# A graph network's first message stage: 555 instead of 491 edge tiles counted, their one-hots made one tile at a time from SBUF, and the stage's side work spread over the counted tiles

## The chip, the core and the metric

The kernel runs on one core of a Trainium2 chip. The metric is the device time of one execution in microseconds, as the median of several runs. Engines are named as the profile names them: PE is the matrix engine (PEld its weight loads), DVE the vector engine, ACT the scalar engine, POOL the GpSimd engine, SP the queue that issues plain transfers.

## What is computed

A graph of 12,500 nodes with 32 features and 200,000 edges, sorted by destination, passes through two message layers:

```python
def _L0_gnn_ref(x, W, b, src, dst):
    out_norm = rsqrt(max(segment_sum(ones, src), 1))
    in_norm = rsqrt(max(segment_sum(ones, dst), 1))
    agg = segment_sum((x * out_norm[:, None])[src], dst)
    return agg * in_norm[:, None] @ W + b

h = maximum(layernorm(x), 0)
x = x + _L0_gnn_ref(h, W, b, src, dst)
h = maximum(layernorm(x), 0)
# per edge: relu MLP of [h_i, h_j - h_i], 64 -> 64 -> 128 -> 64 -> 32, mean over the edges of a destination
x = x + _L1_gnn_ref(h, src, dst, W1, b1, W2, b2, W3, b3, W4, b4)
```

All arithmetic is to float32 accuracy; the first layer keeps it with three bfloat16 terms per value.

## The kernel before

Edges come in tiles of 128 and chunks of four tiles (512 edges); there are 391 chunks. The program is one instruction stream per engine in an order written out by hand (`tc.manual_schedule()`); each engine runs its stream in that order, and waits on the others through semaphores.

**Stage A** (until about 338 us): layer norm, the table `tab_h` of normalized rows, the out-degrees of all nodes, and the scaled table `tab_hn` (three bfloat16 terms and a one per node). Meanwhile POOL gathers the source rows of the first 64 chunks (`EARLY`) from unscaled tables, one indirect transfer for each tile of 128 edges (line 211, the one line that issues all gathers).

**Stage B** (the first layer's sums, until about 1392 us) treats the chunks in three ways:

- The 64 early chunks hold rows without the degree factor. `scale_rows` looks the factor up on chip and adds the chunk: a transfer of `srow`, the compare `sturned` (line 656), twelve small products `look` (674), four `mask` instructions (681), the three bfloat16 terms `rows_scaled` (695, 697), the one-hot `hot_e`, four products (703), and an addition into the sums (562). It is a generator; `advance(running)` moves every running one by one stage per chunk step, and a new one starts every third chunk step (`LATER = 3`).
- Chunks 64 to 267 (below `DIR = 268`) are gathered from `tab_hn` by POOL, four gathers each into one of eight `rows` buffers, one-hots `hot` are made on DVE (624), and `sum_rows` (638) multiplies them on PE.
- The last 491 tiles (`ND`) from chunk 268 on are not gathered at all. `count_edges` makes, for each tile, a matrix of counts (source row within 128 by destination) from two one-hots on PE (786), `lo` and `oh`; ACT copies it from PSUM to SBUF as bfloat16 (788), in two parts, `count_two` and `count_third`, each with a single PSUM buffer; and after eight tiles (`TD`) `multiply` multiplies the on-chip `table` with the eight counts, 98 products (735) spread over the first five tiles of the next eight, then turns, places and adds the result (749, 754, 562).

`oh` is made on DVE for two tiles in one instruction (723): a comparison of `keys`, in SBUF, with `count_h`, which lies in PSUM:

```python
onehots[i // 2] = oh = dp.tile([P, 3, KW, 2], BF16, name="oh", bufs=4)
nc.vector.tensor_tensor(
    oh, keys[:, :, i : i + 2][:, :, None, :].to_broadcast([P, 3, KW, 2]),
    count_h[:, None, :, :].to_broadcast([P, 3, KW, 2]), op=OP.is_equal)
```

A step of the outer loop issues one chunk's gathers, then the steps of `count_edges` that are due (`stages = ND + 2 * TD = 507` spread over `steps = DIR - EARLY - 6 = 198` chunk steps), one step of the early chunks, and `sum_rows` of two chunks before. Node updates (`update_nodes`, some twelve stages each: product with the weights, norm, product with the next layer's weights, and the writes of `tab_j` and `tab_i` by SP) are queued when all edges of four node blocks are summed, and advance by one stage per counted tile.

**Stage C** (the second layer, to the end) can start gathering when the last update has written `tab_j`: 1563 gathers `gj` on POOL, and for each pair of chunks four PE stages `first` to `fourth` with lags of 1, 3, 4 and 5 steps.

Of the kernel before, what the change touches and what calls it, by code (L numbers as in the profile page):

```python
# [57 lines left out]
LATER = 3  # L58
# [6 lines left out]
DIR = 268  # L65
# [19 lines left out]
def gnn_kernel(  # L85
# [59 lines left out]
    keys = early.tile([P, 3, ND + 1], F16, name="keys")  # L145
# [140 lines left out]
    with tc.tile_pool(name="deg", bufs=3) as hp, tc.tile_pool(  # L286
# [105 lines left out]
        base_ps = pp.tile([P, ND], F32, name="base_ps")  # L392
        nc.tensor.matmul(base_ps, ones, base_f, start=True, stop=True)
        drel = hp.tile([P, ND], F32, name="drel", bufs=1)
        nc.vector.tensor_tensor(drel, dst_i[:, DIR * TPC : NTR], base_ps, op=OP.subtract)
        nc.vector.tensor_reduce(bounds[:, 0:1], drel, AX.X, OP.min)
        nc.vector.tensor_reduce(bounds[:, 1:2], drel, AX.X, OP.max)
        key = hp.tile([P, ND], F32, name="key", bufs=1)
        nc.vector.scalar_tensor_tensor(
            key, hl[:, 0, DIR * TPC : NTR], float(WD), drel, op0=OP.mult, op1=OP.add)  # L400
        nc.vector.memset(keys[:, :, ND:], 0.0)
        for k in range(3):
            nc.vector.tensor_scalar(keys[:, k, :ND], key, float(-KW * k), None, op0=OP.add)
# [54 lines left out]
    def update_nodes(pool, pp, q, sums_of):  # L458


        n = min(J, NBLK - J * q)
        at = slice(J * q, J * q + n)
# [8 lines left out]
        for j in range(n):  # L471
            parts_of = sums_of(j)
            for k, (part, w) in enumerate(parts_of):
                nc.tensor.matmul(ps[:, j, :], part, w, start=(k == 0), stop=(k == len(parts_of) - 1))
# [10 lines left out]
        for j in range(n):  # L485
            b = J * q + j
            nc.vector.scalar_tensor_tensor(
                x1[:, b, :], ps[:, j, :D], c[:, j : j + 1], x1[:, b, :], op0=OP.mult, op1=OP.add)
# [20 lines left out]
        ht = hts[q % 2]  # L509
# [8 lines left out]
        r = P * J * q  # L518
# [3 lines left out]
    class Sums:  # L522
# [43 lines left out]
        def block(self, q, j):  # L566
            return self.tiles[q][:, P * j : P * (j + 1)]
# [31 lines left out]
    with tc.tile_pool(name="e0", bufs=8) as sp, tc.tile_pool(name="nu", bufs=1) as np_, tc.tile_pool(  # L599
# [7 lines left out]

        def reached(g):
            return {q for q in (g // (GRP * J), (g + W // STEP - 1) // (GRP * J)) if q < NQ}

        missing = [len([g for g in range(NCH) if q in reached(g)]) for q in range(NQ)]

        def added(chunks):
            for g in chunks:
                for q in sorted(reached(g)):
                    missing[q] -= 1
                    if missing[q] == 0:
                        updates.append(update_nodes(np_, np_ps, q, lambda j, q=q: [(sums.block(q, j), w0t)]))
# [30 lines left out]
        def scale_rows(g):  # L649
# [4 lines left out]
            yield  # L654
            turned = sp.tile([PART, CHUNK], BF16, name="sturned", bufs=2)
            nc.vector.tensor_scalar(turned, row, part_s[:PART], None, op0=OP.is_equal)
            h = rows_early[:, g, :, :D]
            if g < RAW:
# [3 lines left out]
                nc.vector.tensor_sub(h, h, m[:, :, None].to_broadcast([P, TPC, D]))  # L662
                square = sp.tile([P, TPC, D], F32, name="raw_sq", bufs=2)
# [21 lines left out]
            if g < RAW:  # L685
# [4 lines left out]
                scaled, h, 0.0, w[:, :, None].to_broadcast([P, TPC, D]), op0=OP.max, op1=OP.mult)  # L690
            rows = sp.tile([P, TPC, D3], BF16, name="rows_scaled", bufs=2)
# [7 lines left out]
            yield  # L699

            total = ps[:D3, 1]
            for t in range(TPC):
                nc.tensor.matmul(
                    total, rows[:, t, :], hot[:, t // 2, :, t % 2], start=(t == 0), stop=(t == TPC - 1))
            adds.append((g, total))
# [9 lines left out]
        LATE = (TD - 3, TD - 2)  # L715

        def onehots_of(i):

            if i % TPC == 0:
                c = DIR * TPC + i  # L720
                los[i // TPC] = one_hots(dp, hl[:, 1, c : c + TPC], P, "lo", 3)
            onehots[i // 2] = oh = dp.tile([P, 3, KW, 2], BF16, name="oh", bufs=4)
            nc.vector.tensor_tensor(  # L723
                oh, keys[:, :, i : i + 2][:, :, None, :].to_broadcast([P, 3, KW, 2]),
                count_h[:, None, :, :].to_broadcast([P, 3, KW, 2]), op=OP.is_equal)
# [35 lines left out]
        def count_edges():  # L761
# [3 lines left out]
            onehots_of(0)  # L765
            onehots_of(2)
            for i in range(ND):
# [7 lines left out]
                if i % 2 == 0 and i + 4 < ND:  # L775
                    onehots_of(i + 4)
                oh, lo = onehots[i // 2], los[i // TPC]
# [3 lines left out]
                for ranges, name in ((THIRDS[:2], "two"), (THIRDS[2:], "third")):  # L781
# [3 lines left out]
                    for k in range(len(ranges)):  # L785
                        nc.tensor.matmul(  # L786
                            ps[:, k, :w], lo[:, i % TPC // 2, :, i % 2], oh[:, k0 + k, :w, i % 2], start=True, stop=True)
                    nc.scalar.activation(  # L788
                        counts[g][:, t, a:b, :].rearrange("p (k h) d -> p k (h d)", k=len(ranges)), ps[:, :, :w], AF.Copy)
# [10 lines left out]
        LAG = 2  # L800
        steps, stages = DIR - EARLY - 6, ND + 2 * TD
        for m in range(EARLY, DIR + LAG + 1):
# [3 lines left out]

            while adds:
                early, total = adds.pop()
                sums.add(slice(0, D3), STEP * early, total)
                added([early])  # L810
            if EARLY <= m - LAG - 1:
                add_rows(m - LAG - 1)
            i = m - EARLY
            slots = range(stages * i // steps, stages * (i + 1) // steps)
            for slot in slots:
                if next(counting, None) is None:
                    next(updating)
# [4 lines left out]
                advance(running)  # L822
                later, r = divmod(i, LATER)
                if r == 0 and later < EARLY:
                    running.append(scale_rows(later))
# [6 lines left out]
        assert not running and not updates and not any(missing)  # L832
# [4 lines left out]
    with tc.manual_schedule(), tc.tile_pool(name="prep", bufs=3) as prep, tc.tile_pool(name="e1", bufs=3) as ep, tc.tile_pool(name="fn", bufs=2) as fp, tc.tile_pool(  # L837
# [9 lines left out]
        def finish_nodes(q):  # L847
# [14 lines left out]
            for j in range(n):  # L862
                nc.tensor.matmul(po[:, j, :], sums.block(q, j), w4s, start=True, stop=True)  # L863
# [106 lines left out]
        last = 5  # L970
        for m in range(NPAIR + last):
# [170 lines left out]
```

## Time and profile before

| | us |
|---|---|
| median of 3 runs | 4361.06 (4347.4 to 4362.65) |
| profiled execution, own time | 3372.41 |
| its span, first to last instruction | 3370.4 |
| busy: PE, DVE, ACT, POOL | 2513.0, 1812.9, 1115.0, 2501.0 |

The profiled execution is shorter than the median of the runs by 989 us. Durations and waits are read from the profiled one. In its page, the second part shows the span in 40 equal slices of 84 us, one digit for the busy share in tenths; groups of instructions are listed by line with their count, their total and their mean; a wait names the engine that waited, and what released it.

### The profile page before, as it was taken

To read this page: it belongs to the slowest core of one execution; us is meant where nothing else is said; L and a number is where in the kernel's file an instruction comes from. 1 tells how busy PE (TensorE), PEld (TensorE's weight loads), DVE (VectorE), ACT (ScalarE), POOL (GpSimd) and SP (SyncE) were. 2 spreads that over 40 slices of the span, in tenths; PEclk is the share of its full clock that TensorE was granted. 3 is DMA by queue.
4 is the path that set the end of the run, shared out by engine and by line. 5 is a ranking of instruction groups with operands and counts; after the bars stand their busy time and mean duration, and the time that the engine had idled before them with its cause. 6 is when DMAs were issued, how large, how long until landed. Compare 5 with 4: busy or idle time off the path is not lost. (4 is left out here: it accounts for less than half of the span.)

```text
span 3370.4 us, 54101 instructions
## 1 busy us (share of the span) xinstructions
PE 2513.0 (75%) x20860; PEld 1782.4 (53%) x20860; DVE 1812.9 (54%) x4103; ACT 1115.0 (33%) x2029; POOL 2501.0 (74%) x2655
## 2 busy tenths in 40 slices
PE   3772888888888888477777777777776777777777
PEld 2660666667666666245455445445454544555544
DVE  7995788789878887233333333333333333333333
ACT  0002676677666775111212121121222121221121
POOL 7777777777777777477777777777777777777775
PEclk9855899999999999587878787888878787777788
DMA  4113112222222222222222222222222222222221
GB/s 98 15 15 79 27 28 34 31 37 34 34 34 34 33 35 49 44 59 63 59 59 64 60 62 59 63 59 63 59 62 60 59 63 59 63 59 62 60 60 31
DMA packets 234631, 170.64 MB, mean 51 GB/s; under 512 B 156008, under 2 KB 182856, under 8 KB 234368
## 3 DMA queue, kind: packets, MB, share of 16 engines
q0 software_dynamic: 84320, 75.96, 15.1%
q1 hardware_dynamic: 131306, 85.26, 9.7%
q10 hardware_dynamic: 18742, 5.89, 0.9%
q8 instruction: 168, 2.75, 0.3%
q14 instruction: 95, 0.78, 0.1%
HBM read 153.98 MB, written 12.92 MB: 50 GB/s over the span
## 5 line engine op out<-in xcount | busy, mean ns | idle before, releaser
L211 POOL DMA_INDIRECT gj<-tab_j,src_j x1563 | 1474.7, 944 | 506.9 <-issue 421.5
L211 POOL DMA_INDIRECT rows<-tab_hn,src_j x816 | 770.9, 945 | 252.4 <-issue 191.7
L937 DVE TENSOR_TENSOR h<-p,b3n 128x512 f32<-128x512 f32 x196 | 135.2, 690 | 738.2 <-PE p L934 738.2
L788 ACT ACTIVATE count<-count_two 128x858 bf16<-128x858 f32 x491 | 434.7, 885 | 282.0 <-PE count_two L786 255.7
L934 PE MATMUL p<-w3s,h 128*128 128x64 f32 x3128 | 444.7, 302 | 0.2 <-ACT h L926 0.2
L934 PEld LDWEIGHTS p<-w3s,h 128*128 128x128 f32 x3128 | 416.7, 215 | 48.3 <-issue 40.1
L926 ACT ACTIVATE h<-p,b2s 128x1024 f32<-128x1024 f32 x196 | 217.8, 1111 | 662.4 <-PE p L924 662.4
L902 PE MATMUL p<-gj,ident 128*1 128x8 f32 x392 | 39.1, 174 | 505.9 <-DMA gj<-tab_j,src_j 505.9
L735 PE MATMUL st<-count,table 128*128 128x104 bf16 (+1 forms) x6076 | 375.1, 217 | 48.4 <-ACT count L788 22.4
L735 PEld LDWEIGHTS <-table 128*128 128x128 bf16 x6076 | 347.7, 99 | 90.8 <-issue 30.6
L902 PEld LDWEIGHTS p<-gj,ident 128*1 128x1 f32 x392 | 21.7, 80 | 677.6 <-issue 664.1
L914 ACT ACTIVATE h<-p 128x512 f32<-128x512 f32 x196 | 117.0, 597 | 788.9 <-PE p L910 788.9
L723 DVE TENSOR_TENSOR oh<-keys,kept 128x2574 bf16<-128x2574 f16 x246 | 365.1, 1486 | 11.5 <-PE count_third L786 11.4
L952 PEld LDWEIGHTS ps<-hot,h 128*64 128x64 f32 x3126 | 272.4, 190 | 176.5 <-issue 165.1
L786 PE MATMUL count_two<-oh,lo 128*128 128x429 bf16 x982 | 277.3, 364 | 94.0 <-ACT count L788 84.1
L910 PE MATMUL p<-turned,ai 128*64 128x512 f32 x782 | 330.0, 936 | 0.0
L562 DVE TENSOR_TENSOR acc<-acc,ps 64x64 f32<-64x64 f32 (+1 forms) x198 | 44.7, 226 | 526.0 <-PE ps L952 493.4
L952 PE MATMUL ps<-hot,h 128*64 128x128 f32 x3126 | 298.0, 353 | 0.5 <-DVE h L937 0.5
L211 POOL DMA_INDIRECT rows_early<-tab_h,src_j x224 | 216.0, 964 | 71.2 <-issue 50.9
L886 DVE TENSOR_TENSOR turned<-row,kept 128x512 f32<-128x512 f16 x391 | 249.4, 679 | 26.8 <-PE p L910 22.0
L788 ACT ACTIVATE count<-count_third 128x416 bf16<-128x416 f32 x491 | 252.0, 513 | 0.0
L585 DVE TENSOR_TENSOR hot<-rel_h,kept 128x512 f32<-128x512 f16 x391 | 249.1, 678 | 0.0
(201 smaller groups left out, 3017.7 us busy)
## 6 DMA issues: line engine op xcount, KB each, us to landing
row<-rel_row SPq DMA_DIRECT2D x195, 256.0 KB
gj<-tab_j,src_j POOLq DMA_INDIRECT x1563
rows<-tab_hn,src_j POOLq DMA_INDIRECT x816
ai<-tab_i SPq DMA_DIRECT2D x195, 64.0 KB
srow<-hi_row SPq DMA_DIRECT2D x64, 98.0 KB
rows_early<-tab_h,src_j POOLq DMA_INDIRECT x224
tab_j<-nu_aij SPq DMA_DIRECT2D x24, 128.0 KB
tab_i<-nu_aij SPq DMA_DIRECT2D x24, 128.0 KB
```

The lines of the kernel that those rows point to most:

```text
L211: nc.gpsimd.indirect_dma_start(out=tile_ap, out_offset=None, in_=table, in_offset=bass.IndirectOffsetOnAxis(ap=col, axis=0))
L585: nc.vector.tensor_tensor(hot, rel_h[:, g * TPC : (g + 1) * TPC][:, :, None].to_broadcast([P, TPC, W]), lanes_f[:, None, :W].to_broadcast( ...
L723: nc.vector.tensor_tensor(oh, keys[:, :, i : i + 2][:, :, None, :].to_broadcast([P, 3, KW, 2]), count_h[:, None, :, :].to_broadcast([P, 3, ...
L735: nc.tensor.matmul(ps[:, : tiles * WD], table[:, h, :], c[:, :tiles, h, :], start=(h == 0), stop=(h == PART - 1))
L786: nc.tensor.matmul(ps[:, k, :w], lo[:, i % TPC // 2, :, i % 2], oh[:, k0 + k, :w, i % 2], start=True, stop=True)
L788: nc.scalar.activation(counts[g][:, t, a:b, :].rearrange("p (k h) d -> p k (h d)", k=len(ranges)), ps[:, :, :w], AF.Copy)
L886: nc.vector.tensor_tensor(turned, v["row"][:, k], part_f.to_broadcast([P, CHUNK]), op=OP.is_equal)
L910: nc.tensor.matmul(p1[k * HID : (k + 1) * HID].rearrange("p t e -> p (t e)"), v["ai"][:, k], v["turned"][k], start=False, stop=True, skip_ ...
L926: nc.scalar.activation(h2[:, :n], p2[:, :n], AF.Relu, bias=b2s)
L934: nc.tensor.matmul(p3[:, k * TPC + t, :], v["h2"][:, k, t * P : (t + 1) * P], w3s, start=True, stop=True)
L937: nc.vector.tensor_tensor(h3[:, :n], p3[:, :n], b3n[:, None, :].to_broadcast([P, n, HID]), op=OP.max)
L952: nc.tensor.matmul(ps[k * HID : (k + 1) * HID, o : o + W], v["h3"][:, k * TPC + t, :], v["hot"][k][:, t, :], start=(i == 0 and t == 0), st ...
```

## The change

`DIR` goes from 268 to 252: 64 tiles that were gathered are counted. The one-hot `oh` is made for one tile at a time, by a compare of a constant list of numbers in SBUF (`count_s`, 1287 to a partition) with the tile's key as a scalar for each partition; four are made ahead (`AHEAD_OH`), in seven buffers. The early chunks advance one stage per counted tile instead of per chunk step, start every eighth tile, and have more and shorter stages. The two halves of the node group `QD` are updated separately. Once all tiles are counted, five update stages are issued at a time (`QUICK`). In stage C the last pairs run with lags smaller by one.

```diff
-LATER = 3
+LATER = 8
-DIR = 268
+DIR = 252
...
-    keys = early.tile([P, 3, ND + 1], F16, name="keys")
+    key = early.tile([P, ND], F32, name="key")
+    count_s = early.tile([P, 3 * KW], F16, name="count_s")
...
-        base_ps = pp.tile([P, ND], F32, name="base_ps")
-        nc.tensor.matmul(base_ps, ones, base_f, start=True, stop=True)
-        nc.vector.tensor_tensor(drel, dst_i[:, DIR * TPC : NTR], base_ps, op=OP.subtract)
+        for c in range(0, ND, 512):
+            n = min(512, ND - c)
+            base_ps = pp.tile([P, 512], F32, name="base_ps")[:, :n]
+            nc.tensor.matmul(base_ps, ones, base_f[:, c : c + n], start=True, stop=True)
+            nc.vector.tensor_tensor(
+                drel[:, c : c + n], dst_i[:, DIR * TPC + c : DIR * TPC + c + n], base_ps, op=OP.subtract)
...
-            nc.vector.tensor_scalar(keys[:, k, :ND], key, float(-KW * k), None, op0=OP.add)
+            nc.vector.tensor_scalar(
+                count_s[:, KW * k : KW * (k + 1)], count_h[:, :, 0], float(KW * k), None, op0=OP.add)
...
+        units = [(J * q, min(J, NBLK - J * q)) for q in range(NQ) if q != QD] + [(J * QD, J // 2), (J * QD + J // 2, J // 2)]
...
             nc.sync.dma_start(row, bass.AP(
                 tensor=hi_row.tensor, offset=hi_row.offset + g * CHUNK, ap=[[0, PART], [1, CHUNK]]))
             yield
+            yield
             turned = sp.tile([PART, CHUNK], BF16, name="sturned", bufs=2)
...
                 nc.vector.tensor_sub(h, h, m[:, :, None].to_broadcast([P, TPC, D]))
+            yield
+            if g < RAW:
                 square = sp.tile([P, TPC, D], F32, name="raw_sq", bufs=2)
...
                 scaled, h, 0.0, w[:, :, None].to_broadcast([P, TPC, D]), op0=OP.max, op1=OP.mult)
+            yield
             rows = sp.tile([P, TPC, D3], BF16, name="rows_scaled", bufs=2)
...
             hot = one_hots(sp, rel_h[:, g * TPC : (g + 1) * TPC], W, "hot_e", 2)
             yield
+            yield
...
+            yield
             adds.append((g, total))
...
-            onehots[i // 2] = oh = dp.tile([P, 3, KW, 2], BF16, name="oh", bufs=4)
-            nc.vector.tensor_tensor(
-                oh, keys[:, :, i : i + 2][:, :, None, :].to_broadcast([P, 3, KW, 2]),
-                count_h[:, None, :, :].to_broadcast([P, 3, KW, 2]), op=OP.is_equal)
+            onehots[i] = oh = dp.tile([P, 3 * KW], BF16, name="oh", bufs=7)
+            nc.vector.tensor_scalar(oh, count_s, key[:, i : i + 1], None, op0=OP.is_equal)
...
-                if i % 2 == 0 and i + 4 < ND:
-                    onehots_of(i + 4)
+                if i + AHEAD_OH < ND:
+                    onehots_of(i + AHEAD_OH)
...
+        QUICK = 5
         steps, stages = DIR - EARLY - 6, ND + 2 * TD
...
             for slot in slots:
+                while adds:
+                    early, total = adds.pop()
+                    sums.add(slice(0, D3), STEP * early, total)
+                    added([early])
+                if slot == slots[0] and EARLY <= m - LAG - 1:
+                    add_rows(m - LAG - 1)
                 if next(counting, None) is None:
-                    next(updating)
+                    for _ in range(QUICK):
+                        next(updating)
+                later, r = divmod(slot - 3, LATER)
+                if r == 0 and later < EARLY:
+                    running.append(scale_rows(later))
+                advance(running)
...
+        def lags(m):
+            less = min(1, max(0, m - (NPAIR - 6)))
+            return [max(1, lag - less) for lag in (1, 3, 4, 5)]
```

## The prediction

> **What bounds the kernel now.** I read the page first, then its groups, the stretches, POOL's order of time, and PE's.
>
> ```profile
> span 3370.4 us, 54101 instructions
> PE   3772888888888888477777777777776777777777
> DVE  7995788789878887233333333333333333333333
> ACT  0002676677666775111212121121222121221121
> POOL 7777777777777777477777777777777777777775
> ```
>
> POOL is at 7 in every slice but the 17th (1350 to 1430 us). A 7 is its ceiling, as its own order of time shows:
>
> ```profile
> 1359.39 0.94 POOL L211 DMA_INDIRECT rows<-tab_hn,src_j  x1 [0.30 <-issue]
> 1360.63 0.94 POOL L211 DMA_INDIRECT rows<-tab_hn,src_j  x1 [0.30 <-issue]
> 1392.39 0.94 POOL L211 DMA_INDIRECT gj<-tab_j,src_j  x1 [30.81 <-DMA row<-rel_row]
> 1393.64 0.94 POOL L211 DMA_INDIRECT gj<-tab_j,src_j  x1 [0.31 <-issue]
> ```
>
> A gather takes 0.94 us and 0.30 us of issue: one each 1.249 us. So stage B is 816 x 1.249 = 1019 us of POOL, stage C 1563 x 1.249 = 1952 us, and between them POOL stands for 30.8 us, until the last update has written `tab_j`. But POOL isn't alone at its limit. In stage B the busy shares of PE and DVE are as high:
>
> ```profile
> 338.60:1326.70 988.10, 829.27 (x9741) 640.30 (x9742) 819.11 (x2267) 686.47 (x1320) 744.38 (x788) 0.96 0.21 33
> 1361.60:1392.40 30.80, 12.71 (x49) 9.51 (x49) 9.76 (x36) 4.92 (x13) 0.01 (x1) 0.50 0.13 31
> ```
>
> (PE, PEld, DVE, ACT, POOL, then the PE clock: 0.96.) In 988 us PE is busy for 829 and DVE for 819. From the first `count_third` product (323.2) to the last (1326.7) are 490 steps of 2.05 us. POOL offers one step per 1.95 us (198 chunk steps of 5.0 us for 507 steps), so the counting falls behind: `sum_rows` of a chunk comes 0.4 chunks after its gathers at chunk 82 and 7 at chunk 232, near the end of the eight buffers, and at 1117 and 1208 us a gather waits 0.6 and 2.3 us for a buffer. **Stage B has two bounds, a POOL pace and a counting pace, and the change moves 64 tiles from one to the other.** What counts is the counting pace, so I looked for its floor, in undisturbed groups of eight tiles:
>
> ```profile
> 806.74 0.35 PE L786 MATMUL count_third<-oh,lo 128*128 128x416 bf16 x1
> ...
> 814.98 0.54 PE L786 MATMUL count_two<-oh,lo 128*128 128x429 bf16 x2 [0.79 <-ACT count L788]
> 815.39 0.35 PE L786 MATMUL count_third<-oh,lo 128*128 128x416 bf16 x1
> ...
> 819.83 1.15 PE L735 MATMUL st<-count,table 128*128 128x104 bf16 x19 [0.79 <-ACT count L788]
> ...
> 821.20 0.35 PE L786 MATMUL count_third<-oh,lo 128*128 128x416 bf16 x1
> ```
>
> Eight tiles take 821.20 - 806.74 = 14.46 us; the next eight, to 835.48, take 14.28. That is **1.80 us per tile, with no wait for DVE in it**. It is made of PE alone in the first five tiles (three counting products and some 20 `st` products, 1.6 us), of a loop of PE and ACT in three (the single `count_two` buffer: 0.6 us of product, 0.89 of copy, 1.52 in all), and of 2.5 us where a group's products wait for its last copy. The other 0.25 us per tile of the mean are stalls:
>
> ```profile
> L723 DVE TENSOR_TENSOR oh<-keys,kept 128x2574 bf16<-128x2574 f16 x246 | 365.1, 1486 | 11.5 <-PE count_third L786 11.4
> ```
>
> ```profile
> PE st L735 <- DVE acc_d L558: 19.4, 9, 5.0
> ```
>
> DVE makes `oh` in blocks of 1.49 us; an early chunk's `mask` to `hot_e` is some 4 us in one piece (at 1299.8 to 1303.9), and the addition `acc_d` that frees the `st` buffer stands behind it: PE then waits up to 5 us.
>
> **The change part by part.** Times first in the profiled execution.
>
> *64 gathers fewer.* 64 x 1.249 = 80 us less POOL in stage B. Only what the counting pace allows of it is gained.
>
> *64 tiles more, and the one-hots.* Each tile costs the counting pace once. Does it fall to its floor? DVE's part: before, 1.41 us from start to start for two tiles, 0.70 per tile. The nearest row to the new compare is `sturned`, the same operation on 512 numbers in SBUF:
>
> ```profile
> L656 DVE TENSOR_SCALAR sturned<-srow,part_s x64: 343/347/564, 332.1 to 1321.3; 98x512 bf16<-98x512 f16 x64
> ```
>
> A compare by a scalar from PSUM (line 745, 160 numbers) takes 374 ns, 0.21 us beyond one number per cycle; with that, `sturned` leaves 0.135 us for 512, four per cycle. So 1287 numbers take 0.34 + 0.21 = 0.55 us, 0.47 from start to start: 0.23 less per tile. The other end: the Trainium skill, "VectorE: DVE Perf Modes", What auto-detection actually checks, gives the fast modes of one source where the outermost counts are both even or equal; 1287 is odd, but equal on both sides. If it ran at two per cycle, it would be 0.88 us, more than before. I take 0.55, the row of the same form. DVE's sum for eight tiles is then 8 x 0.47 for `oh`, 1.5 for `lo` and `hot`, 4.4 for an early chunk, 2.1 for places, additions and updates: 11.8 us in 14.4. It no longer limits, and its longest piece is about 2.6 us (masks and one `oh`) under four tiles made ahead. The early stages fall on fixed tiles of a group: `look` is issued after the eighth tile's products, where PE waits 0.8 us for ACT anyway; masks, terms and the four products have a tile each. I cost these moves at nothing; if the cover is gone they cost their old stalls, the 0.25 us per tile. The transfers of `srow` are 64 as before, one per eight tiles, issued a tile earlier; SP has room. PE's products read the same columns.
>
> So I take 1.80 us per tile: 555 x 1.80 = 999, the counts end at 323 + 999 = **1322** (before 1327, with 64 tiles less).
>
> *After the counts.* Before, 65.7 us pass from the last count to the first `gj`, as the gathers end at 1361.6 and three updates run one after another behind them (tab_j's writes at 1368.9, 1377.9 and 1388.5: 9 to 10.5 us each). After: the last two groups' products, 13.4 us as at 1326.7 to 1340.1; the update of the last three blocks, 9; the two halves, 7.3 each (10.5 less half of its products and wide instructions, 3.3); and 4 us from SP's issue to the gather. Sum 41. The first `gj` is at **1363** instead of 1392.4: 29 us saved. The early groups' updates lie in the counting (chunk 63 starts at tile 507). Two more writes by SP (0.36 and 0.5 us) lie in it.
>
> *The locks of POOL and DVE.* This is the rule that speaks against the change. At 1112.26 a `sturned` starts, and the gather that starts 0.10 us later takes 1.05 instead of 0.94; a gather under way made another `sturned` 0.53 long (754.12). The Trainium skill, "SBUF — State Buffer", Who interferes with whom, says that a DVE instruction in a two-port mode and GpSimd exclude each other for the whole instruction, and that the old form, one source in PSUM, stays out of it. If each of 555 compares held a gather for its 0.47 us, that were 261 us, and stage B would end near 1540. The trace prices it lower: a gather is delayed only where it starts 0.1 us or more after the compare and before its end less 0.13 us, that is for 0.33 of 1.249 us, by 0.17 on average: 0.04 us per compare, and at most as much again inside the gather: 24 to 42 us. By the trace POOL's part then ends at 338.6 + 939 + 24 to 42 = 1302 to 1320, 3 us later the last sum, 11 us later the first `gj`: 1316 to 1334, still ahead of 1363. So it costs nothing here, as the counting hides it.
>
> *Stage C* has the same 1563 gathers. Its end: 27.2 us pass from the last gather; a round of PE's four stages there is 4.0 us (3350.94 to 3354.95), and one lag less takes one away: -4. *Stage A* gains a product and makes `count_s` in three instructions of about 0.65 us for three of 0.41, under the early gathers: 0, at most 1.
>
> Sum: -29 - 4 = **-33 us**: 3339 of the profiled execution's 3372.41. The median of the runs is 1.293 times that, and no view says where its 989 us lie. If they are outside all of this, the gain stays 33 (4328); if all is stretched alike, 43 (4318); if they lie in the 2635 gathers (0.375 each), POOL alone bounds stage B, and 64 x 1.62 and the shorter gap count: 125 (4236). I take the middle one: **4318**.
>
> **The rivals.**
>
> *POOL becomes the only bound (0.22).* The counting goes below 1.74 us per tile, and the first `gj` comes at 1316 to 1334: with the end, 62 to 80 us saved, 4257 to 4281; the gathers' share of the 989 us leads to the same place or lower. For it: tiles go at 1.52 and 1.62 when nothing else is in the way. Against it: the floor of 1.80 has neither DVE nor POOL in it.
>
> *The counting doesn't speed up (0.28).* One mechanism: PE's order. Each wait of PE for a copy, an addition or an early product holds all tiles behind it, and 64 more pass through it. Decision point: 323 + 555p + 41 - 4 = 1392.4, p = **1.86**. At 1.93, half of the stalls left, it is 40 us slower: 4413; at the old 2.05, 106 slower, 4498. For it: PE's and ACT's work per tile is unchanged, the PE clock falls in stalls (0.96 in the mean), and five update stages in a row make PE wait for short chains. A compare at 0.88 us ends here too. Against: the stalls named above are DVE's, and their pieces become shorter.
>
> *It doesn't do what it says:* the tiles counted in eight-tile groups hide the one-hots anyway, so that only the gathers and the additional tiles count; that is p near 1.86 and no change, and lies between the first two.
>
> **How the numbers follow.** The likeliest case (0.50) is p from 1.76 to 1.85: -55 to -6 us, 4290 to 4353. By 0.5% (22 us, about what a measurement of this kernel can tell from no change) it is faster down from p = 1.825: 0.36 of the 0.50 faster, 0.13 same, 0.01 slower. The POOL case is all faster (0.22). The slow case is 0.24 slower and 0.04 same. Sum: faster 0.58, same 0.17, slower 0.25. The range leaves out a pace above 1.91 (about 0.14) and gains over 120 us: 4240 to 4402.
>
> **What would show it.** `oh` x555 at 0.55 us; the last `count_third` near 1322 with clean groups still at 14.3 us; the first `gj` near 1363, POOL's wait before it under 20 us or spread over waits for `rows` buffers; gathers in stage B mostly at 0.94 us, a quarter longer by up to 0.33; under 25 us from the last gather to the end. Wrong: `oh` at 0.88 us, counts ending after 1353, or groups well below 14 us.

## The result, and the profile after

The changed kernel takes 4358.65 us (median of 14 runs, 4333.5 to 4377.7) against 4352.0 us for the kernel before (14 runs, 4333.2 to 4367.1): a ratio of **1.0011, interval 0.9993 to 1.0028**. That is no change; predicted was 4318 us, a gain of 43 us.

The runs of a batch, before among them, lie together at one of two levels, near 4340 us or near 3380 us: the timed runs above are of the higher, and the profile of before shown ahead of the prediction (3372.41 us) is of the lower. So times and paces are compared at one level below, and both kernels have a profile at each: before_3 (4339.95 us) and before_again (3379.61 us), after_3 (4338.3 us) and after_4 (3378.9 us).

The page of the changed kernel, at the 4340 level:

```profile
span 4356.3 us, 56425 instructions
...
PE   2444277777777777773667777777777777777777
...
DVE  5555456555555555531222223222322222222323
ACT  0000255555555555550111111111111111111112
POOL 7554345445444444455566666666666666666663
```

In stage B (slices 6 to 18) POOL is at 4 to 5, where the page ahead of the prediction had it at 7, and PE stands at 7. That comes with the level and not with the change, as the page of the kernel before at this level, before_3, shows:

```profile
span 4337.9 us, 54101 instructions
...
PE   2444266677767777663577777777777777777778
...
POOL 6555355555555455555666666666666666666663
```

The order of time of POOL in the changed kernel at the turn from stage B to C, by start, duration, engine, line and what the engine waited for:

```profile
1963.44 0.94 POOL L212 DMA_INDIRECT rows<-tab_hn,src_j  x1 [0.30 <-issue]
1990.50 0.94 POOL L212 DMA_INDIRECT gj<-tab_j,src_j  x1 [26.12 <-DVE turned L902]
1991.75 0.94 POOL L212 DMA_INDIRECT gj<-tab_j,src_j  x1 [0.31 <-issue]
```

A gather still takes 0.94 us and 0.30 of issue; what the profile ahead of the prediction hardly had is the waiting between the gathers of stage B. These waits at this level, the kernel before first (engine and tile, what it waited for, us in total, times, longest):

```profile
POOL rows L211 <- PE ps_late L638: 399.2, 118, 7.8
```

and the changed kernel (after_3):

```profile
POOL rows L212 <- PE ps_late L644: 538.1, 166, 7.6
```

POOL stands for 400 to 540 us of a stage of 1490 until PE has summed the rows that occupy its buffers. At the 4340 level POOL is no bound in stage B; PE's order is. The counting itself, from the instructions that read `oh` (min/median/max in ns, first and last start), before_3:

```profile
L786 PE MATMUL count_third<-oh,lo x491: 344/349/552, 498.3 to 1905.7; 128*128 128x416 bf16 x164
L723 DVE TENSOR_TENSOR oh<-keys,kept x246: 1470/1490/1497, 496.0 to 1889.7; 128x2574 bf16<-128x2574 f16 x123
```

and after_3:

```profile
L737 DVE TENSOR_SCALAR oh<-count_s,key x555: 533/554/769, 497.3 to 1915.2; 128x1287 bf16<-128x1287 f16 x185
L798 PE MATMUL count_third<-oh,lo x555: 336/339/554, 498.6 to 1924.4; 128*128 128x416 bf16 x185
```

Before: 1407.4 us for 490 steps, 2.872 us per tile. After: 1425.8 for 554, **2.574 per tile**. So a tile did become 0.30 us cheaper, and the 64 additional ones took it back: to end where 490 steps had ended, 554 steps had to fall to 1407.4 / 554 = 2.540. The last count comes 18.7 us later. Behind it 24.7 us are saved (last count to first `gj`: 82.5 before, 57.8 after), and the first `gj` is at 1982.1 instead of 1988.2. Stage C is then as long as before, 2354 against 2350 us.

### The profile page after: what moved, and what is told of

Read it like the earlier page. It is cut to its first block, busy times and chain, and to the rows that moved or that the text cites. A ratio compares the mean times of both kernels' runs of the same rounds, so it can differ in the third digit from the quotient of the medians.

```text
span 4356.3 us, 56425 instructions
## 1 busy us (share of the span) xinstructions
PE 2992.5 (69%) x21798; PEld 2019.7 (46%) x21798; DVE 1747.1 (40%) x4444; ACT 1188.9 (27%) x2173; POOL 2466.6 (57%) x2591
## 4 chain that ended last, share of the span: by engine, by line
PE 46%; another core or an unknown queue 20%; issue 12%; ACT 10%; DVE 9%; POOL 3%; DMA 1%; ACTq 0%; DVEq 0%; POOLq 0%
PE p L950 9%; ACT count L801 8%; PE p L940 6%; PE count_two L798 5%; PE st L747 5%; PE ps L968 5%; PE p L926 5%; PE p L922 3%; POOL gj L212 3%; DVE lo L326 2%; PE count_third L798 2%; DVE hi L326 1%; PE ps_late L644 1%; DVE hot L587 1%
## 5 line engine op out<-in xcount | busy, mean ns | idle before, releaser
L950 PE MATMUL p<-w3s,h 128*128 128x64 f32 x3128 | 525.2, 328 | 169.6 <-issue 120.8
L950 PEld LDWEIGHTS p<-w3s,h 128*128 128x128 f32 x3128 | 486.1, 240 | 217.7 <-issue 156.9
L798 PE MATMUL count_two<-oh,lo 128*128 128x429 bf16 x1110 | 340.7, 393 | 312.4 <-ACT count L801 276.4
L747 PE MATMUL st<-count,table 128*128 128x104 bf16 (+1 forms) x6860 | 466.7, 224 | 68.7 <-issue 61.3
L747 PEld LDWEIGHTS <-table 128*128 128x128 bf16 x6860 | 419.3, 103 | 107.0 <-issue 80.3
L940 PE MATMUL p<-h,w2s 64*128 64x512 f32 x782 | 386.4, 887 | 79.2 <-issue 67.5
L798 PEld LDWEIGHTS <-lo 128*128 128x128 bf16 x1665 | 166.9, 107 | 447.3 <-issue 394.5
L737 DVE TENSOR_SCALAR oh<-count_s,key 128x1287 bf16<-128x1287 f16 x555 | 310.8, 567 | 51.4 <-remote 27.2
L343 PE MATMUL deg_ps<-hi,lo 128*128 128x98 bf16 x1563 | 183.5, 270 | 199.4 <-issue 140.4
L922 PE MATMUL p<-ident,gj 128*128 128x128 f32 x784 | 200.4, 371 | 116.1 <-issue 115.1
```

The costliest lines, as they stand in the source:

```text
L737: nc.vector.tensor_scalar(oh, count_s, key[:, i : i + 1], None, op0=OP.is_equal)
L747: nc.tensor.matmul(ps[:, : tiles * WD], table[:, h, :], c[:, :tiles, h, :], start=(h == 0), stop=(h == PART - 1))
L798: nc.tensor.matmul(ps[:, k, :w], lo[:, i % TPC // 2, :, i % 2], oh[:, KW * (k0 + k) : KW * (k0 + k) + w], start=True, stop=True)
L922: nc.tensor.matmul(p1[:, t, :], v["gj"][:, t].rearrange("p k c -> p (k c)"), ident, is_transpose=True, start=(t == 0), stop=False, skip_gr ...
L940: nc.tensor.matmul(p2[:, k], w2s[s, :], v["h1"][s, :], start=True, stop=True)
L950: nc.tensor.matmul(p3[:, k * TPC + t, :], v["h2"][:, k, t * P : (t + 1) * P], w3s, start=True, stop=True)
```

## The experiments

The theory after the result: *two bounds*. The new compare and the new order make a counted tile cheaper, and the 64 tiles eat it; the rivals were that compare and order are worth nothing, and that the gain is lost in stage C. Four expectations (a_oldoh, after_again, b_newoh, a_oldoh260) give their numbers mainly for one level, and the run fell on the other, so that these numbers were not put to the test there.

**before_again, before_3: the kernel before, unchanged.**

> The kernel before, unchanged, profiled once more, because its first profiled execution (3372 us) was 989 us shorter than every timed run. If the missing 989 us lie where the profile of the changed kernel shows its waits (TensorE issuing late, its signals coming late), then this profile is near 4350 us; theory 1 (the counting pace bounds stage B and the change made a tile cheaper, and the 64 additional tiles ate that): counting at 2.9 to 3.0 us per tile against 2.6 after, last count near 1940 in both. Theory 2 (neither the compare nor the schedule matters): 2.6 us per tile here too, last count near 1775, and the 165 us are lost elsewhere in stage B or in the gap to C. Theory 3 (gain in B, lost in C): last count after 1990, and stage C shorter here than the 2340 us of the changed kernel.

> The kernel before, profiled beside the next three. [...] Instruction theory: where before takes 4343, TensorE gets its instructions more slowly at regular places, some 965 us over 41,720 TensorE instructions (23 ns each), and the counting pace is 2.75 to 2.9 us per tile; POOL is then nowhere the bound in stage B. Where it takes 3378 it is as in before_again: 2.08.

before_again fell on the lower level, before_3 on the higher. At 4340 the counting pace is 2.87, close to theory 1's 2.9 to 3.0 (its last count, near 1940, comes at 1905.7); theories 2 and 3 (last count at 1775, or stage C longer after) fall. At 3380 it is 2.059, with POOL's gathers at 1.25 us and POOL the later bound.

**a_dir268: the change without its 64 tiles.** Run three times, as a_dir268, a_dir268_2 and a_dir268_3.

```diff
-DIR = 252
+DIR = 268
```

> The changed kernel with its 64 additional counted tiles taken back (491 tiles, 816 gathers in stage B), all else of the change kept. Theory 1: 64 tiles at 2.6 us are not paid: 130 to 170 us faster than before, near 4200. Theory 2 (the new compare and the order of stages are worth nothing, the tiles cost nothing either, POOL or something outside sets the time): within 0.5% of before, 4330 to 4370. Theory 3 (the additional tiles do save POOL's time as intended, and the new schedule loses it): slower than before by 64 gathers, 80 to 120 us, near 4450.

> Compare and order at 491 tiles, measured 32 us (0.9%) slower where before takes 3378, because its gathers are held up by the compares (41.7 us in sum). Where before takes 4340, POOL has slack in stage B: 25 to 40 us faster than before (0.6 to 0.9%), if the 64 tiles are what eats the gain of the other two parts. If instead the compare and the order don't add up (DVE's stalls can be taken away once only): 17 to 23 us, no more than the better of the two alone. If the 64 tiles cost nothing: within 0.2% of before.

> New compare and new order at 491 tiles. With before at 4340: if the 64 tiles are what eats the gain, 20 to 40 us faster than before (0.5 to 0.9%), the first gj 20 to 35 us earlier than the changed kernel's 1990; if the tiles cost nothing there, within 0.2%. With before at 3380: 27 to 32 us slower once more.

All three fell on the 3380 level: 31.7, 27.3 and 29.1 us *slower* than before (1.0094, 1.0082, 1.0084; intervals within 0.0016 of these). At this level theory 1's gain of 150 us isn't there, and its rival's loss is of a third of the size that it gave. What it is, b_newoh shows.

**b_newoh: the compare alone** (491 tiles, old order), at both levels.

```diff
-            onehots[i // 2] = oh = dp.tile([P, 3, KW, 2], BF16, name="oh", bufs=4)
-            nc.vector.tensor_tensor(
-                oh, keys[:, :, i : i + 2][:, :, None, :].to_broadcast([P, 3, KW, 2]),
-                count_h[:, None, :, :].to_broadcast([P, 3, KW, 2]), op=OP.is_equal)
+            onehots[i] = oh = dp.tile([P, 3 * KW], BF16, name="oh", bufs=7)
+            nc.vector.tensor_scalar(oh, count_s, key[:, i : i + 1], None, op0=OP.is_equal)
...
-                            ps[:, k, :w], lo[:, i % TPC // 2, :, i % 2], oh[:, k0 + k, :w, i % 2], start=True, stop=True)
+                            ps[:, k, :w], lo[:, i % TPC // 2, :, i % 2], oh[:, KW * (k0 + k) : KW * (k0 + k) + w], start=True, stop=True)
```

> The kernel before with one thing of the change alone: one compare per tile from SBUF (four ahead) in place of one per two tiles from PSUM; 491 tiles and the old order of stages. Lock theory: POOL is the later of the two bounds at 491 tiles, so the locks show in full: 25 to 40 us slower (0.7 to 1.2%), gathers of stage B longer by some 40 us in sum. Relief theory (DVE is what the counting waits for, and a shorter compare frees it): the same time or up to 15 us faster, as the last gathers wait less for the counting. Order theory (a_dir268's loss came from the new order of stages): within 0.3% of before.

> The compare alone at 491 tiles. Where before takes 4340: 17 us faster again (0.4%). Where it takes 3378: lock theory 25 to 40 us slower, with gathers of stage B longer by some 40 us in sum; relief theory equal or faster.

At 4340 it is 17.0 us faster (0.9957, 0.9944 to 0.9969), at 3380 it is 43.9 us **slower** (1.013, 1.0115 to 1.0145). The second is the lock theory's sign, and a little over its 25 to 40 us. The group of stage B's gathers (count, busy us and mean ns, idle before them), before_again:

```profile
L211 POOL DMA_INDIRECT rows<-tab_hn,src_j x816 | 772.2, 946 | 256.1 <-issue 193.9 <-DMA rows<-tab_hn,src_j 28.4 <-PE count_third L786 11.9
```

and b_newoh_2:

```profile
L212 POOL DMA_INDIRECT rows<-tab_hn,src_j x816 | 820.3, 1005 | 248.8 <-issue 189.7 <-DMA rows<-tab_hn,src_j 35.4 <-PE count_third L784 10.7
```

816 gathers of 1005 instead of 946 ns are 48.1 us more, and the last of them comes 42.8 us later (1408.0 for 1365.2). One such pair in its order of time:

```profile
505.14 0.56 DVE L723 TENSOR_SCALAR oh<-count_s,key 128x1287 bf16<-128x1287 f16 x1
505.24 1.27 POOL L212 DMA_INDIRECT rows<-tab_hn,src_j  x1 [0.30 <-issue]
```

The gather that starts 0.10 us after a compare takes 1.27 instead of 0.94. With the old compare in the new order (a_oldoh, a_oldoh264) the gathers are at 945 and 947 ns: it is the compare that lengthens them.

At 4340 the gathers are lengthened just so (1004 ns in b_newoh), but there POOL waits 337 us for PE's sums in any case, and what shows is that the counts end 24.0 us earlier than in before_3 (1881.7 for 1905.7). Whether that is relief of DVE is not shown: PE's waits for DVE in stage B fall only from 60.5 to 53.8 us. The edit has a second effect that the prediction put at nothing ("PE's products read the same columns"): the columns of `oh` that a product reads now lie side by side, and `count_third` takes 339 ns instead of 349, `count_two` 347 instead of 355 (medians). Over three products that is 0.026 us per tile, or 13 us for 491 tiles, by estimate half of the 24.

**a_oldoh, a_oldoh260, a_oldoh264, a_oldoh268: the order without the compare**, with 555, 523, 507 and 491 tiles. The edit to the changed kernel (also `keys` in place of `key` and `count_s`, and four buffers of `hot` instead of five, to make room; it is `count_h`, not `keys`, that lies in PSUM):

```diff
-            onehots[i] = oh = dp.tile([P, 3 * KW], BF16, name="oh", bufs=7)
-            nc.vector.tensor_scalar(oh, count_s, key[:, i : i + 1], None, op0=OP.is_equal)
+            onehots[i // 2] = oh = dp.tile([P, 3, KW, 2], BF16, name="oh", bufs=4)
+            nc.vector.tensor_tensor(
+                oh, keys[:, :, i : i + 2][:, :, None, :].to_broadcast([P, 3, KW, 2]),
+                count_h[:, None, :, :].to_broadcast([P, 3, KW, 2]), op=OP.is_equal)
...
-DIR = 252
+DIR = 268
```

a_oldoh keeps 252; 268 is a_oldoh268, and the other two have the number in their names.

> The changed kernel (555 tiles, new order of the early stages) with the one-hots made as before, two tiles in one compare against keys in PSUM, 1.49 us each; hot has four buffers instead of five to make room. Theory 1, with the compare as the source of the cheaper tile: 4430 to 4530 (555 tiles at 2.75 to 2.95). Theory 1, with the order of stages as the source: within 0.7% of after. Theory 2: within 0.5% of before.

> Change in its order of stages, but the old compare (no locks) and 523 tiles: the version that the runs so far point to. Lock theory with p = 1.9: 784 gathers at 1.26 to 1.30 end at 1327 to 1360, counts at 1316, first gj 17 to 25 us behind the last gather as in a_oldoh and a_dir268: 1350 to 1380 instead of before's 1397, and 4 us at the end: 20 to 50 us faster than before (0.6 to 1.5%). If the compare from SBUF is what speeds up the counting, p stays near 2.0 and it is within 0.5% of before or slower.

> The version with the old compare, the new order and 523 tiles, measured 8 us (0.2%) under before where before takes 4343. There again: the same. Where before takes 3378: instruction theory takes 21 us of extra cost away, so 25 to 35 us (0.7 to 1.0%) faster; lock theory, too, has it faster (20 to 50 us), and faster than the changed kernel; relief theory (the compare speeds the counting): within 0.5% of before, slower than the changed kernel.

> The new order of the stages (and of the updates and the last lags) alone: 491 tiles and the old compare of two tiles. If the order makes the tile cheaper (a_oldoh260 had 2.70 with 523 tiles, against 2.87 before): on a chip with before at 4340, pace 2.70 to 2.78, 15 to 30 us faster than before (0.4 to 0.7%). If the compare is what counts and a_oldoh260's pace was only the mixture of more tiles to fewer gathers: within 0.2% of before. On a chip with before at 3378: no locks, first gj 15 us nearer to the last gather: 10 to 25 us faster (0.3 to 0.7%) by the first, equal by the second.

> New order, old compare, 507 tiles and 800 gathers. Two bounds that cross: with before at 3380, gathers end at 338.7 + 800 x 1.25 to 1.28 = 1340 to 1363 and counts at 323 + 506 x 1.98 = 1325, first gj at 1366 to 1380 (a_oldoh268: 1384.8): 20 to 30 us faster than before (0.6 to 0.9%). If the bounds are blended, and more tiles only cost (a_oldoh, 555 tiles: 29 us slower): at or above a_oldoh268's 12 us gain, 3370 to 3380. With before at 4340: 8 to 20 us faster (0.2 to 0.5%), as it is 16 tiles from a_oldoh260 (5 and 8 us faster).

At 3380: 555 tiles 28.5 us slower (1.0079, 1.0064 to 1.0094), 491 tiles 11.7 faster (0.9964, 0.9951 to 0.9977), **507 tiles 16.8 faster (0.9944, 0.993 to 0.9957)**, the largest gain at this level, though its interval touches that of 491 tiles. a_oldoh's expectation gave only 4340's numbers, and the level was the other. In a_oldoh264 the gathers are of 947 ns again and end at 1337.9, the counts at 1303.7; its first `gj` at 1376.1 waits 37 us, in which the last updates run one after another behind the gathers. Its gain was put at 20 to 30 us and is a little under. At 4340, 523 tiles are 8.3 and 5.0 us faster (0.998, 0.9968 to 0.9992; 0.9987, 0.9973 to 1.0).

**b_dir260: the kernel before with 32 more tiles.**

```diff
-DIR = 268
+DIR = 260
```

> The kernel before with 32 more counted tiles (523) and nothing else of the change (the base product is cut in two so that it fits a bank). Theory 1: each tile costs its old pace, 2.9 to 3.0 us: about 94 us slower, 4440 to 4450. Theory 2: within 0.5%. Theory 3: faster by 32 gathers, 40 us or more, near 4310.

46.2 us slower at 3380 (1.0139, 1.0123 to 1.0154): 1.44 us for each tile, half of theory 1's 94 us. With the old compare and the old order, the counting is already close behind POOL, and more tiles only cost: POOL waits 99.5 us for PE's sums here. Its pace was not theory 1's 2.9, which belongs to 4340, but 1.997.

**a_dir260: the change with 523 tiles.**

```diff
-DIR = 252
+DIR = 260
```

> The changed kernel with 523 tiles, half way between 491 and 555. If a_dir268 was bound by POOL with its locks (816 gathers at 1.329) and the 555-tile kernel is bound by counting at p, then 784 gathers at 1.329 end at 341 + 1042 = 1383, 18 us earlier than a_dir268's: time 3392. If counting bounds it at 1.9: counts end at 322 + 994 = 1316 and don't matter. If both bounds are blended (each waits for the other in the one program order), it lies at or above the line between its neighbours. Where TensorE's pace alone bounds everything: 32 tiles at the pace of after less than after (60 to 83 us).

At 4340, 11.7 us faster than before (0.997, 0.9956 to 0.9985), where the changed kernel in the same batch is 8.3 slower: 32 tiles cost 20 us, 0.62 each, net of the 32 gathers they save. The expected 60 to 83 us, the tiles' full pace, missed: the pace rises to 2.676, by my reading because PE sums more gathered chunks among fewer counted tiles.

**after_again, after_3, after_4: the changed kernel beside these.**

> The changed kernel, unchanged, in the company of the next three. The run with the change but 491 tiles (a_dir268) had gathers longer by 41.7 us in all in stage B and its last one 35 us later; the run with the old compare (a_oldoh) counted at 1.907 us per tile against 2.08 of the kernel before. Lock theory: the compares from SBUF hold up gathers by 0.085 us each, but in this kernel POOL has slack, so that it doesn't matter; the counting pace decides. If the pace is that of a_oldoh (1.9: the order of stages makes it, the compare nothing), counts end at 1380 and the time is within 0.5% of before's. If the compare also helps (1.80, as predicted), counts end near 1322 and the time is 30 us (0.9%) under before's. If 2.05 as before: 3 to 4% slower.

> The changed kernel beside the kernel before. Instruction theory: the 64 tiles bring 1876 TensorE instructions; at 23 ns each that is 43 us where before takes 4343, and nothing where it takes 3378. So with 8 us more on the first sort of chip, the change must gain some 35 us (1.0%) on the second, as the prediction's sum of 33 has it. Pace theory (the pace stays at 1.9 to 2.05 and the gain isn't there on any chip): 0 to 4% slower on the second sort. Lock theory in its strong form: slower by 20 us or more on the second.

> The changed kernel beside the corners. Where before takes 4340: within 0.2% of before, and 25 to 45 us slower than a_dir268_2 (64 tiles at a net 0.4 to 0.7 us each, the counting bounding stage B and POOL not). Where before takes 3378: the prediction's sum has it 33 us faster; by the pace of a_oldoh (1.92) its counts end at 1385 and it is within 0.5%; as POOL isn't its bound there, the locks don't show in it, and it is faster than a_dir268 by 20 us or more.

At 4340: 8.3 us slower (1.0018, 1.0007 to 1.0028) and 0.9 slower (1.0004, 0.9987 to 1.0021). At 3380: 2.0 us faster (**0.9996, 0.9988 to 1.0004**). after_4's pace, 1.855, lies between the 1.80 of the prediction and the 1.9 of a_oldoh. So the change is worth nothing, within 0.3%, at either level, and the instruction theory, which wanted 35 us at 3380, falls there.

**a_probe: 2560 products more behind everything.**

```diff
+        for k in range(2560):
+            nc.tensor.matmul(probe_ps, probe, probe[:, :104], start=(k == 0), stop=(k == 2559))
```

> The changed kernel with 2560 products of the shape of st (128 x 104, each with its own load of weights) behind everything, in a row and waiting for nothing: 5120 TensorE instructions. Pace of such a row undisturbed: 0.05 us per product as in stage B's st, 140 us or so. Instruction theory: 140 us where before takes 3378; where it takes 4343 a further 23 ns per instruction, 118 us: 260 in all, in regular slow stretches, one each 256 instructions. If the slow chips lose their time in waits between engines, or in the clock, and not in supplying TensorE: 140 to 170 us on both sorts.

```profile
L1016 PE MATMUL probe_ps<-probe x2560: 209/209/210, 4326.8 to 4445.8; 128*128 128x104 bf16 x197
```

At 4340 the row takes 119.0 us, 46 ns for each product with its load; the kernel is 116 us longer than before (1.0264, 1.0225 to 1.0304). The instruction theory had 260 us for this level, and 140 for a row that isn't slowed: it falls here too. (At 3380 the row was not run.)

The runs side by side, difference to before in the same batch (us):

| tiles | compare | order | at 3380 | at 4340 |
|---|---|---|---|---|
| 491 | new | old | +43.9 | -17.0 |
| 491 | old | new | -11.7 | not run |
| 491 | new | new | +31.7, +27.3, +29.1 | not run |
| 507 | old | new | -16.8 | not run |
| 523 | old | old | +46.2 | not run |
| 523 | old | new | not run | -8.3, -5.0 |
| 523 | new | new | not run | -11.7 |
| 555 | old | new | +28.5 | not run |
| 555 | new | new (the change) | -2.0 | +6.7 (result), +8.3, +0.9 |

Which sign a part has depends on which bound is the later one. At 3380 in the new order, the new compare costs 39 us at 491 tiles (-11.7 to +27.3, in one batch), where POOL is the later bound, and gains 30 us at 555 (+28.5 to -2.0, in two batches), where the counting is: in a_oldoh POOL waits 174.9 us for PE's sums. So, too, the 64 tiles cost 40 us with the old compare (-11.7 to +28.5), and gain 29 with the new one (+27.3 to -2.0), as they take 64 gathers from a POOL that the compare has slowed. At 4340, where the counting is the bound throughout, the compare gains 17 us and 32 tiles cost 20. Both sums come out near nothing. That the two cancel so closely at both levels is a matter of sizes; nothing in the runs makes it necessary.

## Why the prediction was wrong, step by step

*What bounds it.* Two bounds in stage B, and a change that moves tiles from one to the other: right at the 3380 level, of which its profile was (where I read POOL below 7 in the 17th slice alone; it is in the last as well, at 5). At the 4340 level, which the forecast was for, there is one, the counting: in before_3 POOL is idle for 750 us before its 816 gathers, 399 of them waiting for PE's sums.

*oh at 0.55 us:* right, 553 ns in the median. The Trainium skill, "VectorE: DVE Perf Modes", What auto-detection actually checks, let an odd outermost count pass if it is equal on both sides; the measured duration agrees.

*DVE stops limiting:* right. PE's waits for DVE in the counting stretch at 3380, before_again:

```profile
PE st L735 <- DVE acc_d L558: 19.4, 8, 5.0
PE count_two L786 <- DVE oh L723: 8.8, 1, 8.8
PE look L703 <- DVE hot_e L624: 8.3, 4, 3.1
PE nu_ps L507 <- DVE nu_h L503: 7.3, 5, 2.2
```

and after_4:

```profile
PE count_two L798 <- DVE oh L737: 1.9, 3, 0.6
PE ps_late L644 <- DVE acc L563: 1.6, 1, 1.6
PE look L714 <- DVE hot_e L630: 1.3, 4, 0.4
```

All of them come to 52.0 us before and 6.7 after. But 52.0 us are 0.11 per tile: of the 0.25 us per tile above the floor, which the prediction put down to DVE's stalls, less than half was that.

*The pace falls to its floor, 1.80:* this is **the step that failed**. In after_4 it is 1.855:

```profile
L798 PE MATMUL count_third<-oh,lo x555: 336/339/554, 322.1 to 1349.6; 128*128 128x416 bf16 x185
```

The counts end at 1349.6, not 1322. The floor itself was even lower than I put it: an undisturbed group of eight takes 13.78 us, 1.72 per tile.

```profile
348.76 0.34 PE L798 MATMUL count_third<-oh,lo 128*128 128x416 bf16 x1
...
362.54 0.34 PE L798 MATMUL count_third<-oh,lo 128*128 128x416 bf16 x1
```

But I took the floor of groups without an update for the mean of all, and put nothing for the updates of nodes, which the change leaves in the counting. PE's own part of them, in the counting stretch of after_4:

```profile
L515 PE MATMUL nu_ps<-w1s,ht 33*128 33x128 f32 x168 | 24.2, 284 | 1.2 <-ACT ht L511 0.2
L508 PE MATMUL nu_ps<-ident,nu_h 128*32 128x128 f32 x88 | 13.2, 272 | 0.8 <-DVE nu_h L504 0.7
L476 PE MATMUL nu_ps<-w0t,acc_t 97*128 97x33 f32 x72 | 8.9, 268 | 0.1
```

With the other three forms of line 476 (8.1, 4.1 and 1.1 us busy) these are 59.6 us, 0.11 per tile. How the pace goes with the updates shows when the trace of after_4 is taken group by group, from the first `count_third` of eight tiles to the first of the next eight. The first group takes 26.6 us. Of the other 68, the 26 without a product of `nu_ps` take 13.93 us on average, the 42 with one 15.12. Per tile that is 1.74, plus 0.09 for the updates (42 x 1.19 / 555), plus 0.02 for the first group: 1.85. The kernel before, in the profile that the prediction was made from, has the same division: 22 groups without an update at 14.93 us, 38 with one at 16.90. The 1.80 was the pace of some groups without, and most groups carry an update. No run took the updates away, so that they are the cause is read from the trace and not shown by an experiment.

At 4340 the same step failed, by much the same share. A tile became 10.4% cheaper there (2.872 to 2.574) and 9.9% at 3380 (2.059 to 1.855). The forecast was 12.2% (2.05 to 1.80), and 554 steps in place of 490 eat 11.6%. The decision point that the second rival named, p = 1.86, is where the kernel landed, and the third rival's words for such a pace, no change, came true.

*41 us from the last count to the first `gj`:* 45.0 at 3380 (65.0 before_again), and at 4340 57.8 instead of 82.5. Right in mechanism; the saving of 24.7 us was forecast, and came to 20.0 and 24.7.

*The locks, 24 to 42 us, hidden by the counting:* in after_4 195 gathers of stage B last over 0.96 us and are 44.0 us longer in all, just above the range. Hidden in the changed kernel, yes: POOL waits 75.8 us for `ps_late` there. The place where they do cost, b_newoh_2, I had not asked about; there 48.1 us of longer gathers stand beside a loss of 43.9. The literal rule of the Trainium skill, "SBUF — State Buffer", Who interferes with whom, a compare's whole length for each, would have been 0.55 x 491 = 270 us; measured are 48. That is 0.10 us for each compare, not my 0.04 to 0.08. That a shared port is the reason is that page's account; the runs show the lengthening, and that the compare brings it.

*Stage C, -4; stage A, 0:* stage A 0 (first `rows` at 338.0 and 338.1). From the start of the last gather to the end, after_4 takes 28.6 us, before_again 28.3: no gain. The same code took 24.5 in a_oldoh268 and 25.6 in after_3, so the shorter lag can show; what kept it back in after_4 wasn't followed.

*The sum and its conversion.* At 3380 the first `gj` comes at 1394.6 instead of 1363: 27.6 of the miss is the counts' end, 4.0 what follows it. before_again's is at 1396.9, so 2.3 us are gained instead of 29. The conversion by 1.293 to the level of the timed runs failed for its own reason: that level isn't the other one stretched. Stage B of before is 1.42 times as long (1498.6 for 1058.8), stage C 1.19 times, a gather's own duration unchanged; and with another bound in stage B, a part of the change can have another sign. I wrote that no view says where the 989 us lie, and then took three ways of spreading a gain over them, of which none had a loss in it. The slow rival, given 0.28, was the one that carried this: "PE's order".

## What to carry to other kernels

When work is moved from one bound to another, cost it on the receiving side by the mean of that stretch with all that shares its engine, not by its cleanest groups: here 42 of 69 groups carried an update and took 1.2 us more than the rest, 0.09 us per tile, over a third of the 0.25 us on which the forecast stood. A cheaper instruction that holds up another engine is a gain or a loss by which of the two is the bound, so look at the pair at the balance where it will run: at 3380 the same compare cost 39 us with 491 tiles and gained 30 with 555. And when a profile and the timed runs don't agree on the total, no sum made in that profile is a forecast of those runs until it is known which engine the difference hits.

The version that the runs point to is the new order with the old compare and 507 tiles (a_oldoh264): 0.56% faster at 3380, against nothing for the change. At 4340 it was not run; its neighbour with 523 tiles is 0.1 to 0.2% faster there.

## What the runs showed of the hardware

*The level.* At 4340 PE has stretches in which it issues an instruction or two each 0.7 us or a multiple of it and waits for nothing that the profile shows. In stage A, where 16 products follow in a row in before_again:

```profile
121.77 1.62 PE L342 MATMUL deg_ps<-hi,lo 128*128 128x98 bf16 x16 [0.40 <-DVE lo L325]
123.85 1.63 PE L342 MATMUL deg_ps<-hi,lo 128*128 128x98 bf16 x16 [0.46 <-DVE lo L325]
```

before_3 has

```profile
148.85 0.34 PE L342 MATMUL deg_ps<-hi,lo 128*128 128x98 bf16 x2 [1.85 <-issue]
150.96 0.25 PE L342 MATMUL deg_ps<-hi,lo 128*128 128x98 bf16 x1 [1.77 <-issue]
151.69 0.27 PE L342 MATMUL deg_ps<-hi,lo 128*128 128x98 bf16 x1 [0.48 <-issue]
```

for some 13 us at a time, and then runs on. The 1563 products of this line take 376 us there instead of 199, and the first `rows` comes 151 us later (489.6 for 338.1). In stage A these stretches are regular: from the 267th product on, one comes every 112 products or so (at 267, 379 and 491), 27 us apart, and in after_3 they begin at nearly the same products (269, 378 and 491). Yet a_probe's row, of 119 us and 2560 products, with no gathers beside it and no waits in it, has no such stretch at the same level, so neither the time that passes nor the number of products alone brings them. Whether it is the gathers' transfers, the waits, or something else stays open; so does why one batch has them and the next has not. Some expectations speak of two sorts of chip; but the records name chip 1 for the batch of after_3, at 4340, and for that of after_4, at 3380, so the chip's number alone doesn't decide the level.

In stage B it is PE's weight loads that stand without a wait that the profile shows (us, times, longest), before_again:

```profile
PEld L786 <- issue: 106.6, 157, 1.4
```

and before_3:

```profile
PEld L786 <- issue: 381.5, 422, 15.7
```

*PE's clock* is lower at 4340 too. Stage B of the kernel before by its stretch (length, then busy us and instructions of PE, PEld, DVE, ACT and POOL, the granted clock, DMA share, GB/s), before_again:

```profile
338.00:1396.00 1058.00, 870.78 (x10052) 674.39 (x10052) 846.10 (x2379) 699.23 (x1354) 772.22 (x816) 0.94 0.21 34
```

and before_3:

```profile
490.00:1988.00 1498.00, 1029.09 (x10070) 762.51 (x10070) 872.34 (x2398) 705.74 (x1364) 771.78 (x816) 0.82 0.15 26
```

DVE, ACT and POOL do the same work in about the same busy time (within 3%); PE's grows by 158 of the 440 us, and the rest is idle time. The clock, 0.94 and 0.82, can stand for the 158 (0.94 / 0.82 = 1.15, PE's busy time grew 1.18 times), not for the rest.
